# A graph-attention loop on one core: edge values and transposes amid TensorE's picks, one subtraction and the next terms an iteration later

## The chip, the core and the metric

The kernel runs on one core of a Trainium2 chip. A core has five engines that run side by side, each with its own queue of instructions in order: TensorE (PE in the profile; PEld is its weight load), VectorE (DVE), ScalarE (ACT), GpSimd (POOL) and SyncE (SP), which issues most of the DMAs. They share an on-chip memory (SBUF) and the accumulator banks of TensorE (PSUM), and wait for each other on semaphores. The metric is the device time of one execution in microseconds (us); it is the median of several runs.

## What is computed

The reference is one layer of attention over a graph with 6,250 nodes and 206,250 edges (sorted by their destination), 64 channels in 4 heads of 16, followed by a residual and a layer norm. Cut to its core:

```python
Qh = (x @ Wq.T + bq).reshape(n, H, D)
Kh = (x @ Wk.T + bk).reshape(n, H, D)
Vh = (x @ Wv.T + bv).reshape(n, H, D)
Ee = (edge_attr @ We.T + be).reshape(-1, H, D)
score = (Kh[src] * Qh[dst] * (1.0 / np.sqrt(D)) * Ee).sum(-1)
score = jnp.exp(jnp.clip(score, -5.0, 5.0))
msg = Vh[src] * score[..., None]
wV = jax.ops.segment_sum(msg, dst, num_segments=n)
x = _layernorm(x + wV.reshape(n, H * D))
```

So each edge needs the key and value row of its source, the query row of its destination and its own edge value; it makes a weight and a message, and the messages are summed at their destinations.

## The kernel before

The edges are cut into 1,612 tiles of 128, and 8 tiles make a group `g`; there are 202 groups. Two groups in a row make a step (the last 8 groups are steps of one). The main loop (L884) runs one iteration per group, and each iteration works on several groups at once, at different stages. The order of all instructions on all engines is written out by hand: each engine runs its own in program order. Adding a call earlier or later in the loop's body is what orders it against others on the same engine; between engines, waits follow from the tiles that are read and written.

The stages of a group, by function. All matmuls are issued through `product` (L690), so they share line L691 in the profile and are told apart by the tile they write.

- `edges` (L693, PE, room<-et): 8 matmuls that multiply edge features with the edge weights, into the upper part of the tile `room`. `biased` (L702, L706, ACT) adds the bias and copies them to SBUF as `eb`.
- `queries` (L709, PE, qq<-to,qw): the query rows of the destinations, by a matmul with one-hot columns that ACT builds (`onehot_rows`, L247, and `onehot_rows_rest`, L253).
- `terms` (L717, L721, DVE): query times edge value, `term`. `turn` (L723, L727, PE): its four transposes, into the tile `qe[g % 2]`.
- `products` (L742, DVE): L745 multiplies the keys with `qe`, L748 adds up per head: the score.
- `weigh` (L751, ACT): L754 and L756 clip and exponentiate it. The weights of a group are written into `room` as well.
- `message` (L758, L768, DVE): value times weight, written over `qe[g % 2]`. As the sums are to be exact in bfloat16 matmuls, the message is split into three parts: `keep` (L780, L782, ACT) copies what is left to bfloat16, `take` (L784, L787, DVE) subtracts that copy. So per group: keep 0, take 0 (the first subtraction, qe<-qe,msg), keep 1, take 1 (the second, msg<-qe,msg, which is the third part).
- `sums` (L799, PE, room<-msg,of): 16 matmuls, once per step, in even iterations, add the messages of a step at their destinations through a one-hot matrix (`onehot_edges`, L729, L737, DVE), into the `pa` part of `room`. `add` (L818, DVE, odd iterations): L822 adds the three parts up, L828 twice adds the sum to the node rows.

`room` (L615) is one PSUM tile of two banks. Edge values, sums, and the weights lie in it side by side, and accesses of different engines to it are ordered as accesses to the whole tile.

Key and value rows of the sources come in two ways. Most are gathered by POOL, one indirect DMA a tile (`gather`, L264, 1,320 in the run, 128 rows each). A batch of four tiles in about three iterations is fetched on TensorE instead: `hots` (L647, L651, DVE) makes one-hot blocks, `picks` (L661, PE, pick<-hot,parts) multiplies them with the table, three matmuls of 128x512 for each of 25 blocks. An iteration has 24 or 27 picks (33 blocks in four iterations). When a batch is complete, `picked` (L671, L673, DVE) masks it, `picked_kv` (L676, PE) multiplies it with the key and value weights and `place_kv` (L683, L686, ACT) copies it to its place. `by_two` (L656) gives the blocks of an iteration in twos. `mark` and `where` note matmuls of the iteration; the iteration's gathers are made to wait for these, spread over them.

In iteration `g` the order was, on each engine:

- PE: edges of g + 3, [picked_kv], all picks, transposes of g + 1, queries of g + 2, [sums, if g is even]
- DVE: products of g, first piece of one-hots, message of g, other pieces, first subtraction of g, [add, if g is odd], [picked], [one-hots of the step, if g is odd], second subtraction of g, terms of g + 2
- ACT: weights of g (L754, L756), bias of g + 3, L247, first copy of g, [place_kv], L253, second copy of g

The lines that set the order around the picks:

```python
                if g + 3 < NG:
                    edges(g + 3)
...
                for some in by_two(todo):
                    picks(some)
                    where.append(mark[-1])
                if g + 1 < NG:
                    turn(g + 1)
                if g + 2 < NG:
                    queries(g + 2)
```

The functions that the change touches, and what calls them:

## Time and profile before

| | before |
|---|---|
| median of 3 runs | 2070.77 us (2070.09 to 2071.17) |
| the profiled execution's own time | 2091.55 us |
| its span in the profile | 2089.7 us |
| mean granted TensorE clock | 0.946 |
| DVE, largest groups (busy) | L651 469.5, L768 139.9, L748 138.3, L787 139.3 and 137.0, L721 137.1, L745 137.2 us |
| PE, largest groups (busy) | picks 1110.1, sums 159.5, edge values 151.8, transposes 126.0 us |
| POOL | 1,320 gathers, 1248.4 us busy |
| DMA | 97 GB/s to and from HBM over the span |

The profile is one execution, recorded by the hardware; its time lies somewhat above the runs without a profile. A row of the timeline has the start, the duration, the engine, the line, the operation with what it writes and reads, its size, and in brackets how long the engine had been idle before it and what seems to have released it ("issue" where nothing recorded did). "xN" joins N instructions in a row into one line. The view of waits adds up such idle time by waiter and releaser. The view of windows gives, for a stretch of time, its length, each engine's busy time in it, the granted clock of TensorE as a share of full speed, the share of the DMA engines' time and GB/s. The ends of matmuls are modelled, so the start of the next is the better mark.

### The profile page before, as it was taken

How to read it: one execution, taken by the hardware profiler on the slowest of the kernel's cores; microseconds unless marked ns; L12 is line 12 of the kernel's file. 1: busy time of each engine (PE TensorE's matmuls, PEld its weight loads, DVE VectorE, ACT ScalarE, POOL GpSimd, SP SyncE). 2: the span in 40 equal slices, each digit the busy share in tenths (PEclk: the TensorE clock that was granted, in tenths of full speed). 3: DMA queues.
4: the chain of work that ended last, by engine and by line, in shares of the span. 5: the costliest groups of instructions: out<-in, count | busy, mean ns of one | idle time of the engine just before them, and what ended most of it. 6: DMA issues, size and time to landing. Idle time of an engine off the chain costs nothing.

```text
span 2089.7 us, 29080 instructions
## 1 busy us (share of the span) xinstructions
PE 1715.4 (82%) x9720; PEld 881.7 (42%) x9907; DVE 1563.1 (75%) x2484; ACT 995.5 (48%) x1712; POOL 1287.9 (62%) x1370
## 2 busy tenths in 40 slices
PE   6488798888888888888878888888888888878864
PEld 6244344444444444444434444444444443444432
DVE  5377777777777787777777778777877777778775
ACT  3454454445444455445444454444444544445553
POOL 6566666666666666666666666666666666666552
PEclk9789999999999999999999999999999999999975
DMA  6534333333333333333333333333333333333320
GB/s 174 191 92 117 89 99 100 84 101 101 81 102 85 102 97 86 102 92 102 100 82 100 96 93 102 83 99 102 82 111 90 98 101 82 101 87 95 95 81 24
DMA packets 115175, 203.87 MB, mean 98 GB/s; under 512 B 55427, under 2 KB 56175, under 8 KB 114901
## 3 DMA queue, kind: packets, MB, share of 16 engines
q1 hardware_dynamic: 71058, 112.94, 18.2%
q0 software_dynamic: 43520, 87.91, 16.5%
q8 instruction: 80, 1.31, 0.3%
q10 hardware_dynamic: 436, 1.04, 0.2%
q14 instruction: 81, 0.66, 0.1%
HBM read 194.18 MB, written 7.59 MB: 97 GB/s over the span
## 4 chain that ended last, share of the span: by engine, by line
PE 60%; DVE 14%; issue 11%; ACT 10%; another core or an unknown queue 2%; POOL 1%; DMA 1%; DVEq 0%; POOLq 0%; ACTq 0%; SPq 0%
PE pick L691 44%; PE room L691 12%; DVE hot L651 4%; ACT eb L706 3%; DVE qe L768 3%; DVE qe L787 2%; PE qe L727 2%; PE qq L691 1%; ACT room L756 1%; ACT to L253 1%; ACT to L247 1%; PE ps L467 1%; ACT msg L782 1%; POOL kv L264 1%
## 5 line engine op out<-in xcount | busy, mean ns | idle before, releaser
L264 POOL DMA_INDIRECT kv<-kv_tab,src_i x1320 | 1248.4, 946 | 747.1 <-issue 295.2
L691 PE MATMUL pick<-hot,parts 128*128 128x512 bf16 x4538 | 1110.1, 389 | 100.3 <-issue 88.0
L691 PEld LDWEIGHTS <-parts 128*128 128x128 bf16 x4725 | 455.2, 100 | 724.9 <-issue 270.6
L651 DVE TENSOR_TENSOR hot<-from,still 128x2560 bf16<-128x2560 bf16 (+4 forms) x411 | 469.5, 1149 | 0.0
L754 ACT ACTIVATE score<-score,five_p 128x32 f32<-128x32 f32 x202 | 64.9, 321 | 756.0 <-DVE score L748 419.8
L768 DVE SCALAR_TENSOR_TENSOR qe<-room,kv 128x512 f32<-128x512 f32 x200 | 139.9, 699 | 273.4 <-ACT eb L706 243.3
L691 PE MATMUL room<-et,we_sb 64*64 64x256 f32 (+1 forms) x1616 | 151.8, 428 | 141.3 <-DVE qe L787 33.0
L782 ACT ACTIVATE msg<-qe 128x512 bf16<-128x512 f32 x400 | 236.9, 592 | 7.0 <-DVE qe L787 4.3
L253 ACT ACTIVATE to<-to,one_p 126x1024 bf16<-126x1024 bf16 x198 | 227.3, 1148 | 0.0
L691 PE MATMUL room<-msg,of 128*128 128x192 bf16 x1592 | 159.5, 254 | 81.0 <-issue 26.9
L247 ACT ACTIVATE to<-kb,minus_row 126x1024 bf16<-126x1024 uint8 x198 | 224.8, 1135 | 0.0
L721 DVE TENSOR_TENSOR term<-eb,qq 128x512 f32<-128x512 f32 x202 | 137.1, 679 | 115.1 <-PE pick L691 35.3
L787 DVE TENSOR_TENSOR msg<-qe,msg 128x512 bf16<-128x512 f32 x200 | 137.0, 685 | 65.0 <-issue 28.0
L691 PEld LDWEIGHTS <-of 128*128 128x128 bf16 x1600 | 136.5, 101 | 107.8 <-issue 79.4
L756 ACT ACTIVATE room<-score,five_p 128x32 f32<-128x32 f32 x202 | 58.8, 291 | 232.4 <-PE pick L691 180.0
L706 ACT ACTIVATE eb<-room,be_col 128x512 f32<-128x512 f32 x202 | 138.6, 686 | 25.6 <-remote 15.9
L787 DVE TENSOR_TENSOR qe<-qe,msg 128x512 f32<-128x512 f32 x200 | 139.3, 696 | 6.9 <-ACT msg L782 3.6
L748 DVE TENSOR_REDUCE score<-prod 128x32 f32<-128x512 f32 x202 | 138.3, 684 | 7.0
L745 DVE TENSOR_TENSOR prod<-kv,qe 128x512 f32<-128x512 f32 x202 | 137.2, 679 | 5.3 <-issue 2.7
L727 PE MATMUL qe<-ident,term 128*128 128x128 f32 x806 | 126.0, 280 | 5.3 <-DVE term L721 4.9
L691 PEld LDWEIGHTS room<-et,we_sb 64*64 64x64 f32 x1616 | 49.1, 138 | 191.8 <-issue 125.9
L727 PEld LDWEIGHTS qe<-ident,term 128*128 128x128 f32 x806 | 102.7, 144 | 49.0 <-DVE term L721 9.6
(139 smaller groups left out, 972.5 us busy)
## 6 DMA issues: line engine op xcount, KB each, us to landing
et<-in_eT SPq DMA_DIRECT2D x100, 512.0 KB
kb<-key_tab SPq DMA_DIRECT2D x101, 252.0 KB
kv<-kv_tab,src_i POOLq DMA_INDIRECT x1320
srcs<-in_src_rows SPq DMA_DIRECT2D x63, 256.0 KB
qw<-q_tab SPq DMA_DIRECT2D x202, 15.8 KB
kv_tab<-kv_sb SPq DMA_DIRECT2D x4, 640.0 KB
q_tab<-q SPq DMA_DIRECT2D x5, 480.0 KB
y<-in_x_blocks SPq DMA_DIRECT2D x2, 512.0 KB
```

Source lines behind the costliest of these rows:

```text
L247: nc.scalar.activation(TO[g][:, :n, :], KB.pop(g)[:, :n * P].rearrange("p (j e) -> p j e", j=n), AF.Square, bias=minus_row3[:3 * W])
L253: nc.scalar.activation(TO[g][:, :n, :], TO[g][:, :n, :], AF.Relu, bias=one_p[:3 * W], scale=-1.0)
L264: return nc.gpsimd.indirect_dma_start(out=kv_of(g)[:, j, :], out_offset=None, in_=kv_tab[:, :], in_offset=bass.IndirectOffsetOnAxis(ap=src ...
L651: nc.vector.tensor_tensor(HOT[k][:, :hi - lo].rearrange("p b (a c) -> p b a c", c=2), pairs(FROM[m])[:, None].to_broadcast(shape), block2[ ...
L691: mark.append(nc.tensor.matmul(*aps, **kw))
L706: nc.scalar.activation(EB[g][:, :n].rearrange("p (i r) e -> p r i e", r=2), ee[:, :, :n // 2], AF.Identity, bias=be_col)
L727: nc.tensor.transpose(qe[g % 2][:, k:k + half + 1:half, :], TERM[g][:, k, :], ident)
L745: nc.vector.tensor_mul(prod[:, :n, :], kv_of(g)[:, :n, :C], qe[g % 2][:, :n, :])
L748: nc.vector.tensor_reduce(score, prod[:, :n, :].rearrange("p g (h d) -> p g h d", h=H), axis=AX.X, op=OP.add)
L768: nc.vector.scalar_tensor_tensor(to.rearrange("p g (h d) -> p g h d", h=H), WEIGHT.pop(g)[:, :, :, None].to_broadcast([P, n, H, D]), LEAST ...
L782: nc.scalar.activation(part, left, AF.Copy)
L787: nc.vector.tensor_sub(left if i == 0 else part_of(g, 2)[1], left, part)
```

## The change

In the loop, the order of the calls changes; the functions stay as they are.

- On PE, four blocks (12 picks) come first, then the edge values of g + 3, the transposes of g + 1 and the queries of g + 2, then the remaining picks, then the sums. `picked_kv`, where there is one, comes ahead of all.
- On DVE, after the products of g come the second subtraction of group g − 1 and the terms of g + 1, then the first piece of one-hots. The first subtraction of g comes last in the iteration, behind the add and the step's one-hots.
- On ACT, the second copy of g − 1 opens the iteration, ahead of the weights. The bias is added to the edge values of g + 2, computed an iteration before.
- Ahead of the loop, the groups 0 to 2 are prepared as this order needs it.

```diff
-            for g in range(2):
-                edges(g)
-                biased(g)
-                queries(g)
-                terms(g)
+            edges(0)
+            biased(0)
+            queries(0)
+            terms(0)
             turn(0)
+            edges(1)
+            biased(1)
+            queries(1)
             edges(2)
-            biased(2)
...
                 parted = now and step_of[g] < WHOLE
+                former = before and step_of[g - 1] < WHOLE
                 fetch_blocks(g)
                 where.append(mark[-1])
-                if g + 3 < NG:
-                    edges(g + 3)
+                if former:
+                    keep(g - 1, 1)
                 if now:
                     products(g)
+                if former:
+                    take(g - 1, 1)
+                if g + 1 < NG:
+                    terms(g + 1)
+                if now:
                     weigh(g)
-                if g + 3 < NG:
-                    biased(g + 3)
+                if g + 2 < NG:
+                    biased(g + 2)
                 for mc in ahead[:1]:
                     hots(*mc)
...
                 for mc in ahead[1:]:
                     hots(*mc)
-                if parted:
-                    take(g, 0)
                 for s in done:
                     add(s)
...
-                for some in by_two(todo):
+                two = by_two(todo)
+                for some in two[:2]:
                     picks(some)
                     where.append(mark[-1])
+                if g + 3 < NG:
+                    edges(g + 3)
                 if g + 1 < NG:
                     turn(g + 1)
                 if g + 2 < NG:
                     queries(g + 2)
+                for some in two[2:]:
+                    picks(some)
+                    where.append(mark[-1])
                 where.append(mark[-1])
                 if g - 1 in ends and now:
                     sums(ends[g - 1])
                 if g + 4 < NG:
                     onehot_rows_rest(g + 4)
-                if parted:
-                    keep(g, 1)
...
                 if parted:
-                    take(g, 1)
-                if g + 2 < NG:
-                    terms(g + 2)
+                    take(g, 0)
```

## The prediction

> **What bounds the kernel now.** I read the page first, then the list of waits, then the timeline of one pair of iterations, then windows of it.
>
> ```profile
> span 2089.7 us, 29080 instructions
> PE 1715.4 (82%) x9720; PEld 881.7 (42%) x9907; DVE 1563.1 (75%) x2484; ACT 995.5 (48%) x1712; POOL 1287.9 (62%) x1370
> PE 60%; DVE 14%; issue 11%; ACT 10%; another core or an unknown queue 2%; POOL 1%; DMA 1%; DVEq 0%; POOLq 0%; ACTq 0%; SPq 0%
> L691 PEld LDWEIGHTS <-parts 128*128 128x128 bf16 x4725 | 455.2, 100 | 724.9 <-issue 270.6
> L782 ACT ACTIVATE msg<-qe 128x512 bf16<-128x512 f32 x400 | 236.9, 592 | 7.0 <-DVE qe L787 4.3
> ```
> ```profile
> L768 DVE SCALAR_TENSOR_TENSOR qe<-room,kv x200: 698/700/700, 105.7 to 2069.6; 128x512 f32<-128x512 f32 x100
> ```
> PE carries 60% of the chain of waits, DVE 14% and ACT 10%: PE is the bound, but a handshake with the other two adds to it. L768 runs once an iteration: (2069.6 − 105.7)/199 = 9.87 us, 19.74 us a pair (odd iteration, then even). The loop has 4725 picks, in the code 33 × 3 in four iterations, or 24.75 each: 4725/49.5 = 95 full pairs.
>
> ```profile
> DVE qe L768 <- ACT eb L706: 243.3, 105, 6.6
> POOL kv L264 <- PE pick L691: 239.7, 194, 2.4
> ACT room L756 <- PE pick L691: 180.0, 88, 5.7
> ```
> Here (waiter, releaser: total us, times, longest) is the handshake. L756, which writes the weights into the tile `room`, waits 2.0 us a time (180.0/88) for a PE signal, and L768 then waits 2.3 (243.3/105) behind it. The timeline of one pair shows why (start, duration, what; the idle time before in brackets):
>
> ```profile
> 1061.04 0.41 PE L691 MATMUL qq<-to,qw 126*64 126x512 bf16 x2
> 1061.37 1.49 PE L691 MATMUL room<-msg,of 128*128 128x192 bf16 x16
> 1062.80 0.66 PE L691 MATMUL room<-et,we_sb 64*64 64x256 f32 x8
> 1063.12 0.69 DVE L721 TENSOR_TENSOR term<-eb,qq 128x512 f32<-128x512 f32 x1 [0.24 <-PE room L691]
> ...
> 1063.72 0.68 DVE L745 TENSOR_TENSOR prod<-kv,qe 128x512 f32<-128x512 f32 x1
> ...
> 1064.44 0.69 DVE L748 TENSOR_REDUCE score<-prod 128x32 f32<-128x512 f32 x1
> 1065.04 1.48 DVE L651 TENSOR_TENSOR hot<-from,still 128x2560 bf16<-128x2560 bf16 x1
> ...
> 1067.62 0.29 ACT L756 ACTIVATE room<-score,five_p 128x32 f32<-128x32 f32 x1 [2.14 <-PE pick L691]
> ...
> 1067.94 0.69 ACT L706 ACTIVATE eb<-room,be_col 128x512 f32<-128x512 f32 x1
> ...
> 1068.66 0.70 DVE L768 SCALAR_TENSOR_TENSOR qe<-room,kv 128x512 f32<-128x512 f32 x1 [2.14 <-ACT eb L706]
> ...
> 1069.27 0.94 DVE L651 TENSOR_TENSOR hot<-from,still 128x1536 bf16<-128x1536 bf16 x1
> ...
> 1070.19 0.70 DVE L787 TENSOR_TENSOR qe<-qe,msg 128x512 f32<-128x512 f32 x1
> ...
> 1070.80 0.35 DVE L822 TENSOR_REDUCE room<-room 128x64 f32<-128x192 f32 x1
> ...
> 1071.39 0.28 DVE L828 SCALAR_TENSOR_TENSOR y<-room,below,y 128x64 f32<-128x64 f32 x1
> ...
> 1071.81 0.66 PE L691 MATMUL room<-et,we_sb 64*64 64x256 f32 x8 [1.33 <-DVE qe L787]
> 1072.40 4.86 PEld L691 LDWEIGHTS <-parts 128*128 128x128 bf16 x24 [0.38 <-issue]
> ...
> 1077.60 0.60 PE L727 MATMUL qe<-ident,term 128*128 128x128 f32 x4
> ...
> 1078.12 0.76 PE L691 MATMUL qq<-to,qw 126*64 126x512 bf16 x2
> ...
> 1078.58 0.29 ACT L756 ACTIVATE room<-score,five_p 128x32 f32<-128x32 f32 x1 [2.19 <-PE pick L691]
> ...
> 1080.38 1.48 PE L691 MATMUL room<-msg,of 128*128 128x192 bf16 x16 [1.49 <-DVE qe L768]
> 1081.79 0.66 PE L691 MATMUL room<-et,we_sb 64*64 64x256 f32 x8
> ```
> The edge values (room<-et) take 0.59 to the next PE work (1071.81 to 1072.40), so in the odd iteration they end at 1063.39; yet L756, which needs them, starts at 1067.62, 4.23 later; in the even iteration they end at 1072.40 and L756 starts at 1078.58, 6.2 later. This late arrival I call the lag. From L756 the chain L706, L768, hot, L787, sum, add takes 1071.81 − 1067.62 = 4.19 to the next edge values, which may not overwrite the tile before. Lag and chain together just outlast the 24 picks: PE idles 1.33 there, and 1.49 before the sums for L768. The lag is not constant:
>
> ```profile
> 1980.27 0.66 PE L691 MATMUL room<-et,we_sb 64*64 64x256 f32 x8
> ...
> 1982.29 0.29 ACT L756 ACTIVATE room<-score,five_p 128x32 f32<-128x32 f32 x1
> ```
> ```profile
> 1972.00:2000.00 28.00, 27.79 (x173) 14.62 (x174) 24.18 (x36) 14.70 (x26) 11.18 (x12) 1.00 0.33 87
> 1200.00:1600.00 400.00, 340.08 (x1965) 170.57 (x2003) 313.32 (x479) 197.46 (x330) 252.92 (x268) 0.97 0.35 97
> ```
> Near 1980, with POOL's gathers sparse (11.18 us busy of 28), L756 starts 2.02 after the edge values' start, 1.4 after their end, and waits for nothing: PE is busy 27.79 of 28. Over 1200 to 1600, POOL is busy 63% and PE 85%.
>
> **The change part by part.** No instruction is added or removed; the built order keeps each kind's count. What moves:
>
> *Edge values amid the picks.* Before, edge values open the iteration, with 24 picks of cover for the L756–L828 chain. Now 12 picks come first, then edge values (g+3), transposes, queries, and 12 or 15 more picks. They must still wait for the add (odd iterations) or L768 (even). One pick takes (1077.60 − 1072.40)/24 = 0.217 us, so the cover falls from 5.2 to 2.60 us. Edge values 0.59 (1071.81 to 1072.40), transposes 0.52 (1077.60 to 1078.12), queries 0.35 (by starts, 1061.04 to 1061.37): 1.46. Later picks 12.75 × 0.217 = 2.76. Sums 1.43 (1061.37 to 1062.80).
>
> *L756 no longer needs this iteration's edge values.* In an even iteration these are half an iteration old: free. In an odd one L756 now follows the sums, the last PE work of the iteration before, on the same tile. What queues behind L756 on ACT: L706, L247, the first bfloat16 copy L782; DVE's L768 waits for it, and all behind L768, the add included, which releases the edge values. So the chain keeps its PE signal, from sums instead of edge values, 1.5 us earlier, while its end is needed at 12 picks instead of 24.
>
> *First subtraction last.* L787 (0.61, 1070.19 to 1070.80) leaves the chain between L768 and add: 4.19 − 0.61 = 3.58.
>
> *Second subtraction and terms an iteration later.* They go to DVE behind the products: L787 0.61 and L721 0.60 (1063.12 to 1063.72), ahead of the first hot. The sums and transposes that need them come over 2.6 us later; no wait there. The products L745 now wait for transposes issued in the middle of the previous iteration; behind L745 stands all of DVE.
>
> *The rest.* Bias L706 moves to older edge values, the second copy ahead of L754 on ACT: 48% busy, hidden by DVE's products; without that cover 0.59, a copy's 592 ns, an iteration. Gathers wait on other marks of PE's order; none is added, and POOL is 62% busy; SP's DMAs keep their order. Cost nothing.
>
> *The lag's price.* No row shows L756 waiting for sums. Bounds: 1.4 (1980) and 6.2 (even row). From the sums' end (1062.86, start plus duration) to L756's start stand 4.76, between the odd row's 4.23 and 6.2: I take 4.76. For transposes to L745 the nearest row is queries' end 1061.45 to L721 at 1063.12: 1.67; bounds 0.3 (in the sparse window, an estimate from PE busy 27.79 of 28: no wait is left) and 6.2.
>
> *Sum.* Odd iteration, from the end of the sums: 4.76 + 3.58 = 8.34 to edge values, where 12 picks cover 2.60; PE stalls 5.74. Then 1.46 + 2.76: 12.56. Even iteration: the transposes ended 0.35 + 2.76 = 3.11 before it starts; DVE starts 1.67 after them, then L745 0.72, L748 0.60, L787 0.61, L721 0.60, hot 1.40 (1.48 less the 0.08 by which starts overlap), L768 0.70, signal 0.14 (1071.67 to 1071.81): 6.44 − 3.11 = 3.33 to edge values (cover 2.60, stall 0.73), then 1.46 + 2.76 + 1.43: 8.98. Pair 21.54 against 19.74: +1.80, times 95 = +171 us. The quoted pair (1062.80 to 1081.79) takes 18.99, 0.75 under the mean, for batches' products and source work that I take as lost in the stall; if not, +71 more. The profiled execution took 2091.55 us (span 2089.7 and 1.85 around it), 20.78 over the median 2070.77; the difference carries over: 2070.8 + 171 = 2242.
>
> **The rivals.** *Signals on time, faster.* The pair is 7.80 + lag of the sums, plus 7.31 + lag of the transposes (at least its own work, 6.82 + 1.43 = 8.25, as soon as that lag is under 0.94). It beats 19.74 when the two lags sum to less than 4.63 (6.43 taken). Halved, 2.38 and 0.84: 10.18 + 8.25 = 18.43, −1.31 × 95 = −124: 1946. For: 1972 to 2000; sums are earlier than edge values were. Against: POOL's 63% in the long window, and L756's lag of 4.23 and 6.2 in a common pair.
>
> *The clock falls.*
> ```profile
> 1095.52 1.13 PE L691 MATMUL room<-et,we_sb 64*64 64x256 f32 x8 [3.08 <-DVE room L822]
> 1096.59 8.19 PE L691 MATMUL pick<-hot,parts 128*128 128x512 bf16 x26
> 1104.62 0.60 PE L727 MATMUL qe<-ident,term 128*128 128x128 f32 x4
> ```
> ```profile
> 1096.00:1098.00 2.00, 2.00 (x12) 0.59 (x5) 2.00 (x4) 0.00 (x0) 1.39 (x3) 0.50 0.37 61
> ```
> After 3.08 idle the granted clock is 0.50: 27 picks took 8.03, 0.297 each, and edge values 1.13 instead of 0.66. An odd stall of 5.74 would bring it each pair: 12.75 × 0.08 = 1.02 on the later picks, 0.47 on edge values, about 0.5 on transposes and queries (the same ratio, an estimate): 2.0 × 95 = +190: 2432. Against: the sum's stall is an average, and the lag may shrink first. The Trainium skill, "TensorE: Matmul & The Clock Gate", section "What's actually happening", puts the fall to half rate after an idle window of about 3.4 us and the return after about as much sustained work; the row agrees, at 3.08 us, and by that rule 2432 would be the time.
>
> *The lag shrinks as POOL gets room.* POOL's gathers are fixed, so a longer iteration leaves it more idle; with lags of 4.0 and 1.2, 11.80 + 8.51 = 20.31, +0.57 × 95 = +54: 2125. For: the contrast of the two windows.
>
> *The change doesn't do what it says* (no edge values moved, no wait changed): the built order shows both moved; within 0.2%.
>
> **How the numbers follow.** Forecast (2170 to 2330): 0.42. Clock (to 2450): 0.20. Smaller lag (2075 to 2170): 0.16. Faster (1850 to 2066): 0.18. No change: 0.04. A measurement tells 0.2%, 4 us, from nothing: faster 0.18, same 0.04, slower 0.78. The range leaves out the faster half of the fast case and the tail of the clock's: 2000 to 2430; the likeliest one's own range is 2170 to 2330.
>
> **What would show it.** Right: an odd iteration near 12.6 us and an even one near 9; PE idle 4 to 6 us before the odd edge values, released by the add; L756 in odd iterations released by the sums. Wrong: L756 starting within 3 us of the sums' end; L745 late by more than 3 us; a mean granted clock well under 0.95 (then the clock's rival); PE's busy share over 82%.

## The result, and the profile after

The changed kernel takes 2097.38 us (median of 4 runs, 2095.77 to 2100.46) beside 2070.97 us for the kernel before (2070.09 to 2071.64): a ratio of 1.013, 95% interval 1.0112 to 1.0147. It is 26 us slower; 171 us were forecast. A ratio can differ a little from that of the medians, since it leaves out executions in a slower state (one of four of the kernel without marks below). Two more comparisons of the same two kernels gave 1.0151 (1.013 to 1.0173) and 1.014 (1.0118 to 1.0162).

The page of the profile of the kernel after, its first lines, the chain by engine, and three groups (busy, mean ns; idle time just before, and what ended it):

```profile
span 2095.1 us, 29075 instructions
PE 1754.0 (84%) x9907; PEld 875.6 (42%) x9907; DVE 1546.8 (74%) x2484; ACT 1020.4 (49%) x1712; POOL 1287.9 (61%) x1370
...
PE 65%; DVE 18%; ACT 7%; issue 7%; another core or an unknown queue 1%; DMA 1%; POOL 0%; ACTq 0%; SPq 0%; DVEq 0%; POOLq 0%
...
L691 PE MATMUL pick<-hot,parts 128*128 128x512 bf16 x4725 | 1139.3, 396 | 0.7 <-issue 0.4
...
L745 DVE TENSOR_TENSOR prod<-kv,qe 128x512 f32<-128x512 f32 x202 | 138.3, 685 | 358.5 <-PE pick L691 250.8
L691 PE MATMUL room<-et,we_sb 64*64 64x256 f32 (+1 forms) x1616 | 146.8, 435 | 277.9 <-ACT to L253 90.2
```
The same three groups in the kernel before (the record of 187 of its picks is missing from the trace):

```profile
L691 PE MATMUL pick<-hot,parts 128*128 128x512 bf16 x4538 | 1110.1, 389 | 100.3 <-issue 88.0
...
L691 PE MATMUL room<-et,we_sb 64*64 64x256 f32 (+1 forms) x1616 | 151.8, 428 | 141.3 <-DVE qe L787 33.0
...
L745 DVE TENSOR_TENSOR prod<-kv,qe 128x512 f32<-128x512 f32 x202 | 137.2, 679 | 5.3 <-issue 2.7
```
The stalls changed place. Ahead of the products L745 stood 5.3 us in the whole run before, now 358.5; ahead of the edge values 141.3, now 277.9; ahead of picks 100.3, now 0.7. The waits of the kernel after (waiter, releaser: us in total, times, longest):

```profile
POOL kv L264 <- PE pick L691: 330.9, 213, 8.0
...
DVE prod L745 <- PE pick L691: 250.8, 107, 5.4
...
PEld room L691 <- DVE qe L768: 114.5, 56, 6.0
ACT room L756 <- PE room L691: 111.1, 52, 3.9
...
DVE qe L768 <- ACT eb L706: 34.5, 25, 6.7
```
L768 behind L706 has all but gone (243.3 to 34.5); L756 waits for `room` (the sums) in place of the picks that followed the edge values. Both are as the prediction has them. The size is not, and the timeline of one pair shows where (start, duration, what, idle time before):

```profile
1058.91 0.66 PE L727 MATMUL qe<-ident,term 128*128 128x128 f32 x4
...
1059.83 3.41 PE L691 MATMUL pick<-hot,parts 128*128 128x512 bf16 x15
1060.38 0.94 POOL L264 DMA_INDIRECT kv<-kv_tab,src_i  x1 [0.30 <-issue]
...
1062.67 0.69 DVE L745 TENSOR_TENSOR prod<-kv,qe 128x512 f32<-128x512 f32 x1 [3.97 <-PE pick L691]
...
1063.02 0.94 POOL L264 DMA_INDIRECT kv<-kv_tab,src_i  x1 [1.70 <-PE pick L691]
1063.08 1.48 PE L691 MATMUL room<-msg,of 128*128 128x192 bf16 x16
...
1064.40 2.75 PE L691 MATMUL pick<-hot,parts 128*128 128x512 bf16 x12
...
1064.66 0.29 ACT L756 ACTIVATE room<-score,five_p 128x32 f32<-128x32 f32 x1 [0.23 <-ACT score L754]
...
1066.59 0.69 DVE L768 SCALAR_TENSOR_TENSOR qe<-room,kv 128x512 f32<-128x512 f32 x1
...
1068.64 0.28 DVE L828 SCALAR_TENSOR_TENSOR y<-room,below,y 128x64 f32<-128x64 f32 x1
...
1069.02 0.66 PE L691 MATMUL room<-et,we_sb 64*64 64x256 f32 x8 [1.86 <-ACT to L253]
...
1070.50 0.94 POOL L264 DMA_INDIRECT kv<-kv_tab,src_i  x1 [0.31 <-issue]
1070.53 4.86 PEld L691 LDWEIGHTS <-parts 128*128 128x128 bf16 x24 [0.23 <-issue]
...
1073.02 0.69 DVE L745 TENSOR_TENSOR prod<-kv,qe 128x512 f32<-128x512 f32 x1 [2.03 <-PE pick L691]
...
1073.40 0.94 POOL L264 DMA_INDIRECT kv<-kv_tab,src_i  x1 [1.95 <-PE pick L691]
...
1077.68 0.66 PE L691 MATMUL room<-et,we_sb 64*64 64x256 f32 x8 [1.79 <-DVE qe L768]
```
The sums end at 1064.40, where the picks begin, and L756 starts 0.26 later; 4.76 was taken. The odd stall is 1.86, not 5.74. (The releaser named there, L253, is the last to finish by the profile; the edge values wait for the add, which ends at 1068.92, and follow it by 0.10.) The products do come late: 3.1 us after the transposes in the first iteration (1059.57 to 1062.67), 2.75 in the second (1070.27 to 1073.02). Both times they start within 0.4 us of a gather that had waited for TensorE too.

Over groups 10 to 189 the waits that the prediction priced are, in mean us, worked out from each record's start and end in the trace (the two iterations of a pair apart):

```
                                     before          after
                                  odd    even     odd    even
edge values' end to L756         4.34    5.22      -       -
sums' end to L756                  -       -     0.71      -
transposes' end to L745          4.21    4.82     2.22    2.45
L756 behind L748's end           1.92    1.22     2.18    0.43
L768 to the next edge values     3.48    3.20     2.69    1.23
stall ahead of edge values       1.15    0        1.62    0.95
```
The last row is the stall ahead of the edge values that come next after the iteration's L768. In 73 of the 90 odd iterations of the kernel after, L756 starts more than 0.25 us behind L754, so with these late signals, too, it mostly waits for the sums. From the first picks of an iteration to those of the next, an odd iteration takes 9.56 us and an even one 10.48; 12.56 and 8.98 were forecast.

Where TensorE's own time went, from the start of the first pick to the end of the last (each group up to the start of the next; "between" is idle time of over 0.1 us between groups, and "inside" is such idle time within groups, which their columns contain):

```
          picks  edge v. transp. queries  sums  batches  between    sum   inside
before   1170.9    135.5   101.5    75.0  150.8    94.0    166.5  1894.3   104.5
after    1119.5    122.9   126.9    74.0  141.1    81.3    242.9  1908.7    10.4
```
Idle time between groups rose by 76 us, and idle time inside them fell by 94. Without any idle time TensorE's work takes 32 us more, 25 of it in the transposes. That makes 14 us. The medians differ by 26; the profiled execution of the kernel before lay 20.6 us above its median, the one after within its runs. The gain inside the groups is not the clock's:

```profile
200.00:1900.00 1700.00, 1471.93 (x8429) 715.83 (x8428) 1285.52 (x1978) 835.45 (x1367) 1068.36 (x1132) 0.94 0.35 95
```
```profile
200.00:1900.00 1700.00, 1445.93 (x8329) 724.98 (x8493) 1309.59 (x1989) 819.99 (x1375) 1074.79 (x1138) 0.97 0.35 95
```
After, then before; the third number from the end is the granted clock, and it is lower after the change. By the trace's record of the clock it fell to half 58 times in the run after and 33 times before. In these 1,700 us TensorE was at work at half clock for 190 us after and 93 before, which costs at most half of that time, 95 and 47 us.

### The profile page after: what moved, and what is told of

It is laid out like the page before. It is cut to its first block, busy times and chain, and to the rows that moved or that the text cites. A ratio compares the mean times of both kernels' runs of the same rounds, so it can differ in the third digit from the quotient of the medians.

```text
span 2095.1 us, 29075 instructions
## 1 busy us (share of the span) xinstructions
PE 1754.0 (84%) x9907; PEld 875.6 (42%) x9907; DVE 1546.8 (74%) x2484; ACT 1020.4 (49%) x1712; POOL 1287.9 (61%) x1370
## 4 chain that ended last, share of the span: by engine, by line
PE 65%; DVE 18%; ACT 7%; issue 7%; another core or an unknown queue 1%; DMA 1%; POOL 0%; ACTq 0%; SPq 0%; DVEq 0%; POOLq 0%
PE pick L691 43%; PE room L691 11%; PE qe L727 6%; DVE hot L651 5%; PE qq L691 3%; DVE prod L745 3%; DVE score L748 3%; DVE qe L768 2%; DVE msg L787 2%; DVE term L721 2%; ACT to L253 2%; ACT to L247 2%; ACT eb L706 1%; ACT msg L782 1%
## 5 line engine op out<-in xcount | busy, mean ns | idle before, releaser
L691 PE MATMUL pick<-hot,parts 128*128 128x512 bf16 x4725 | 1139.3, 396 | 0.7 <-issue 0.4
L691 PEld LDWEIGHTS <-parts 128*128 128x128 bf16 x4725 | 461.1, 101 | 586.1 <-issue 142.4
L745 DVE TENSOR_TENSOR prod<-kv,qe 128x512 f32<-128x512 f32 x202 | 138.3, 685 | 358.5 <-PE pick L691 250.8
L691 PE MATMUL room<-et,we_sb 64*64 64x256 f32 (+1 forms) x1616 | 146.8, 435 | 277.9 <-ACT to L253 90.2
L782 ACT ACTIVATE msg<-qe 128x512 bf16<-128x512 f32 x400 | 237.6, 594 | 275.9 <-DVE qe L787 127.0
L754 ACT ACTIVATE score<-score,five_p 128x32 f32<-128x32 f32 x202 | 64.9, 321 | 519.5 <-DVE score L748 468.0
L253 ACT ACTIVATE to<-to,one_p 126x1024 bf16<-126x1024 bf16 x198 | 226.6, 1144 | 0.0
L768 DVE SCALAR_TENSOR_TENSOR qe<-room,kv 128x512 f32<-128x512 f32 x200 | 138.8, 694 | 101.1 <-issue 42.3
L727 PE MATMUL qe<-ident,term 128*128 128x128 f32 x806 | 151.2, 317 | 15.9 <-issue 13.2
L691 PE MATMUL room<-msg,of 128*128 128x192 bf16 x1592 | 155.3, 250 | 10.4 <-issue 9.9
L756 ACT ACTIVATE room<-score,five_p 128x32 f32<-128x32 f32 x202 | 58.8, 291 | 186.0 <-PE room L691 111.1
L706 ACT ACTIVATE eb<-room,be_col 128x512 f32<-128x512 f32 x202 | 138.6, 686 | 22.2 <-PE room L691 8.0
L748 DVE TENSOR_REDUCE score<-prod 128x32 f32<-128x512 f32 x202 | 138.3, 684 | 7.0
L727 PEld LDWEIGHTS qe<-ident,term 128*128 128x128 f32 x806 | 96.3, 156 | 103.3 <-issue 99.9
```

What stands on the lines that cost most here:

```text
L253: nc.scalar.activation(TO[g][:, :n, :], TO[g][:, :n, :], AF.Relu, bias=one_p[:3 * W], scale=-1.0)
L691: mark.append(nc.tensor.matmul(*aps, **kw))
L727: nc.tensor.transpose(qe[g % 2][:, k:k + half + 1:half, :], TERM[g][:, k, :], ident)
L745: nc.vector.tensor_mul(prod[:, :n, :], kv_of(g)[:, :n, :C], qe[g % 2][:, :n, :])
L748: nc.vector.tensor_reduce(score, prod[:, :n, :].rearrange("p g (h d) -> p g h d", h=H), axis=AX.X, op=OP.add)
L768: nc.vector.scalar_tensor_tensor(to.rearrange("p g (h d) -> p g h d", h=H), WEIGHT.pop(g)[:, :, :, None].to_broadcast([P, n, H, D]), LEAST ...
```

## The experiments

Each experiment ran beside the kernel before, on the same chip. Four of the six comparisons, the one of the result among them, had the kernel before at 2070 to 2092 us; in the other two the very same program took 1728.8 and 1729.7 us. I call these "with the lag" and "without the lag", for reasons that the experiments give; all ratios are to the kernel before in the same comparison. Lines in profiles of edited kernels can be one or two lower than in the tables above.

### Parts of the change (with the lag, before 2092.1 us)

TensorE's part alone:

```diff
-                if g + 3 < NG:
-                    edges(g + 3)
...
-                if g + 3 < NG:
-                    biased(g + 3)
...
-                for some in by_two(todo):
+                two = by_two(todo)
+                for some in two[:2]:
                     picks(some)
                     where.append(mark[-1])
+                if g + 3 < NG:
+                    edges(g + 3)
+                    biased(g + 3)
                 if g + 1 < NG:
                     turn(g + 1)
                 if g + 2 < NG:
                     queries(g + 2)
+                for some in two[2:]:
+                    picks(some)
+                    where.append(mark[-1])
```


> Only TensorE's order is changed: the first 12 picks, then edge values (with their bias behind them on ACT), transposes, queries, then the other picks; DVE and ACT keep the order of the kernel before, so the first subtraction is still ahead of the add. Theory A (cover: what the change costs is the cover, 12 picks instead of 24 for the chain from L756 to the add): the whole of the cost and more, since the 0.61 us of the first subtraction is in the chain, 0.61 x 95 = 58 us above the changed kernel, near 2155 us. Theory B (the lag of TensorE's signals depends on when the gathers pause, not on the signal): L756 waits for no edge values of its own iteration any more, so it starts on time, and the kernel is between before and after, 2060 to 2100 us.

Measured: 2256.96 us, 1.0805 (1.0771 to 1.0839). Both theories missed. Its waits name the reason:

```profile
DVE msg L787 <- ACT msg L782: 488.4, 174, 7.9
...
ACT eb L706 <- PE pick L691: 260.1, 53, 7.7
```
The bias still belongs to the edge values of the same iteration, which now come in the middle of the picks. ACT stands at L706 for their late signal, the second copy L782 stands behind it, and DVE stands at the second subtraction (488.4 us in all). So the moves are not a sum of parts. In the whole change the bias belongs to older edge values and the second copy comes an iteration later; without these two, edge values amid the picks cost far more. Which of the two counts, no run tells.

DVE's and ACT's part alone, TensorE in its old order (bias stays at g + 3, with a third `eb` buffer):

```diff
+                if former:
+                    keep(g - 1, 1)
                 if now:
                     products(g)
+                if former:
+                    take(g - 1, 1)
+                if g + 1 < NG:
+                    terms(g + 1)
+                if now:
                     weigh(g)
...
-                if parted:
-                    take(g, 0)
...
-                if parted:
-                    keep(g, 1)
...
                 if parted:
-                    take(g, 1)
-                if g + 2 < NG:
-                    terms(g + 2)
+                    take(g, 0)
```


> Only DVE's and ACT's order is changed: second copy, second subtraction and terms an iteration later, first subtraction last; TensorE keeps its order (edge values, all picks, transposes, queries), bias and edge values stay as in the kernel before. Theory A (cover): the chain from L756 to the add is 0.61 us shorter with the full cover of 24 picks, and faster by what the stall ahead of odd edge values allows, up to 0.61 x 95 = 58 us: 2013 to 2060 us. Theory B: L756 still waits for edge values that arrive with the gathers' pause, 4 to 5 us late; the 1.2 us moved ahead of the one-hots are hidden by that, so 2030 to 2075 us. Against both: products wait for the transposes at the end of the iteration before, and then 1.2 us more stand between them and the message: slower, over 2090 us.

Measured: 2087.29 us, 0.9972 (0.9959 to 0.9985): 5 us faster. The odd stall fell from 1.15 to 0.84 us, about half of the 0.61 us that left the chain. This part of the change alone is a small gain.

### The lag taken away (before 2092.1 us)

```diff
-        return nc.gpsimd.indirect_dma_start(
-            out=kv_of(g)[:, j, :], out_offset=None, in_=kv_tab[:, :],
-            in_offset=bass.IndirectOffsetOnAxis(ap=src_i[:, t:t + 1], axis=0))
+        return nc.sync.dma_start(out=kv_of(g)[:, j, :], in_=kv_tab[t % 40 * P:t % 40 * P + P, :])
```
In the kernel before:

> The kernel before with each of the 1,320 gathers on GpSimd replaced by a plain DMA of 128 consecutive rows of the same table to the same place, issued by SP (so the rows are the wrong ones; waits and bytes stay). Theory B (TensorE's signals are late because gathers run back to back): edge values to L756 under 1 us, TensorE busy over 95%, about 8.3 us an iteration as in the window from 1972 to 2000 us: 2071 - 200 x 1.55 = about 1760 us. Rival (the lag belongs to TensorE's signals as such): lag of 4 to 5 us stays and the time is within 3% of 2071.

In the kernel after:

> The changed kernel with the same replacement of its 1,320 gathers. Theory B: no lag, so the odd stall is 0.3 + 3.58 - 2.60 = about 1.3 us a pair and the rest is TensorE's own work: 1.3 x 95 = up to 120 us above the kernel before with the same replacement, or less where the picks of a batch cover it: 1760 to 1880 us. Rival (the lag belongs to the signals): within 3% of 2097.

Measured: 1741.45 us, 0.8321 (0.8303 to 0.8338), and 1810.86 us, 0.8654 (0.8639 to 0.8668). Both kernels came out near theory B's times (about 1760, and 1760 to 1880 us). The lag needs the gathers: without them, L756 follows L748 in 0.39 us in odd iterations of the kernel before (1.92 with them), and TensorE is busy nearly throughout (before, plain rows; engine busy, share of the span):

```profile
PE 1614.3 (93%) x9720; PEld 864.1 (50%) x9907; DVE 1555.8 (89%) x2484; ACT 995.2 (57%) x1712; POOL 39.4 (2%) x50
```
And with no lag, the change costs 69 us (1810.86 − 1741.45), more than with it. Waits of the kernel after, plain rows (L754 is here the line that writes the weights):

```profile
ACT room L754 <- PE room L689: 263.0, 100, 3.3
```
and one odd iteration of it:

```profile
905.61 1.48 PE L689 MATMUL room<-msg,of 128*128 128x192 bf16 x16
907.15 2.54 PE L689 MATMUL pick<-hot,parts 128*128 128x512 bf16 x11
907.20 0.29 ACT L754 ACTIVATE room<-score,five_p 128x32 f32<-128x32 f32 x1 [2.65 <-PE room L689]
...
910.57 0.28 DVE L826 SCALAR_TENSOR_TENSOR y<-room,below,y 128x64 f32<-128x64 f32 x1
...
910.95 0.66 PE L689 MATMUL room<-et,we_sb 64*64 64x256 f32 x8 [1.26 <-ACT to L253]
```
The weights wait 2.65 us for the sums, 0.05 us behind whose end they start. From there to the edge values 3.75 us pass, and 12 picks cover 2.6 of them. In all 100 odd iterations the weights wait for the sums. This is the stall that the prediction describes, at a lag of almost nothing. Idle time on TensorE is 35 us in the loop of the one kernel and 105 in that of the other.

### No marks for the gathers

```diff
             ins = gather_kv(g, j)
-            if j == js[0]:
-                behind(ins, after)
```
In the kernel after:

> The changed kernel with the gathers waiting for no mark in TensorE's order any more; they wait only for their own data and place. Theory B (signals come in when a train of gathers pauses, and the pauses are made by the marks): with no marks the gathers run on until the place they write is still read, the pauses fall elsewhere and less often, and TensorE's signals come later: slower than the changed kernel by 1 to 5%. Rival (only the number of gathers counts, not where they pause): within 0.5% of the changed kernel.

In the kernel before:

> The kernel before with the gathers waiting for no mark in TensorE's order. Theory B: as with the changed kernel, slower by 1 to 5%, with edge values to L756 longer than the 4.3 to 5.2 us of before. Rival: within 0.5% of before.

Measured without the lag (before 1728.77 us): 1797.49 us, 1.040 (1.0383 to 1.0418), and 1730.08 us, 1.0006 (0.9996 to 1.0015). There the marks do nothing, although the gathers run and run back to back. So gathers alone don't make the lag; something else must be added, which the profiles don't show. It is not the chip alone: the comparison of the parts, with the lag, and the last one below, without it, are both on record under the same chip number, 7. The run of the kernel before was repeated where the lag is:

> The kernel before with gathers that wait for no mark, a second time, for a chip with the lag (without it 1.0006 times before). If the pauses that the marks make let TensorE's signals through, there are fewer of them and signals come later: 1.01 to 1.05. If the marks' pauses only hold the gathers up and set the pace, the time falls: 0.95 to 0.99. If neither, within 0.5%.

Measured with the lag (before 2071.55 us): 2367.44 us, 1.1365 (1.1316 to 1.1414): far over the worst expected. Its waits and a piece of its timeline:

```profile
POOL kv L264 <- DVE qe L766: 629.0, 127, 10.5
```
```profile
1203.46 0.94 POOL L264 DMA_INDIRECT kv<-kv_tab,src_i  x1 [2.08 <-DVE qe L766]
...
1212.20 0.94 POOL L264 DMA_INDIRECT kv<-kv_tab,src_i  x1 [0.30 <-issue]
...
1214.92 0.29 ACT L754 ACTIVATE room<-score,five_p 128x32 f32<-128x32 f32 x1 [5.48 <-remote]
...
1216.94 0.94 POOL L264 DMA_INDIRECT kv<-kv_tab,src_i  x1 [3.79 <-DVE qe L766]
```
Eight gathers run in one train from 1203.46 to 1213.14. The weights, which wait for TensorE, start 1.8 us after its end, and the next train waits for their message. The signal came in the pause.

One mark an iteration:

```diff
-                    gather((lot, where[i * len(where) // len(going)]))
+                    gather((lot, where[0]))
```


> The kernel before with both lots of an iteration's gathers behind the first mark, the last matmul of the iteration before, so one wait an iteration instead of two. With the lag, if each pause costs the pace of the gathers about 1.3 us and there are 1.2 an iteration: 6.53 x 1.25 + 1.3 = 9.5 us an iteration, 0.96 of before. If it is the signals that count, they come once an iteration instead of 1.2 times: 1.00 to 1.03. On a chip without the lag: within 0.5%.

Measured with the lag: 2237.62 us, 1.0795 (1.0753 to 1.0836). Both forecasts missed. The "two" of the expectation is mistaken: in the kernel before each gather has a mark of its own, six to eight an iteration. So the series is: a mark for each gather 1, one for an iteration 1.08, none 1.137. Holding the gathers up is not what costs. That too few pauses do fits the series, and is argued: between 150 and 1950 us the gathers run in 227 trains (runs without a pause) in the kernel before, in 139 with one mark and in 142 with none.

TensorE's semaphore events in the trace bear on this. They are fewer than its signals (1,877 for 2,037 in the kernel before), so they are a sample. Counted by where they fall, between 150 and 1950 us (to 1600 without the lag; a train is a run of gathers less than 1.6 us apart, its slots are 1.25 us long, a pause begins 1.9 us after the last gather's start): events for each us spent in that place

```
                             slot 1     2     3     4     5     6     7   8 on  pause
before, with the lag           0.76  1.26  0.63  0.35  0.35  0.24  0.15   0.13   5.08
after, with the lag            0.96  1.09  0.64  0.52  0.30  0.41  0.38   0.19   5.04
before, no marks, with         0.33  0.42  0.52  0.29  0.23  0.24  0.17   0.11   1.04
before, no marks, without        -     -     -     -     -     -     -    0.77     -
before, a mark moved, without    -     -     -     -     -     -     -    1.21     -
```
With the lag, events come at the start of a train, hardly at its end, and in numbers in the pause: in the kernel before 801 of 1,694 fall into 158 us of pauses. Without the lag the gathers hardly ever pause, and events come all the same (the last row is the kernel before with one mark moved, from the last section of experiments).

The place in a train does not decide alone whether a signal is late. In the kernel after, the sums end 1.25 to 2.5 us into a train in 36 of the 90 odd iterations, and L756 follows after 0.25 us in the mean. In the kernel before, the edge values end at the same place in 21 of 90, and L756 follows after 6.18 us, behind the train's end. Why the one signal passes and the other does not is open.

### The weights in a tile of their own

```diff
-            weights = [room[:, 1, 2 * P + C + k * G * H:2 * P + C + (k + 1) * G * H]
-                       .rearrange("p (g h) -> p g h", g=G) for k in range(3)]
+            weights = [accp.tile([P, G, H], F32, name=f"weight{k}") for k in range(3)]
```
In the kernel after, without the lag:

> The changed kernel with the weights in a tile of their own in SBUF, so that L756 waits neither for the sums nor for edge values, and edge values no longer wait for L768. Theory C (what the change costs is the wait of L756 for the sums on the shared tile, 2.2 us behind L748 in odd iterations instead of 0.4, with 12 picks of cover behind it): 1.8 us less in the odd chain and no even stall, 1 to 2 us a pair: 95 to 190 us faster than the changed kernel, 1.00 to 0.92 of the kernel before. Rival (the pace of the gathers and their pauses sets the iteration): stalls only move, within 1% of the changed kernel.

and with the add moved up behind the terms:

```diff
                 if g + 1 < NG:
                     terms(g + 1)
+                for s in done:
+                    add(s)
                 if now:
                     weigh(g)
...
-                for s in done:
-                    add(s)
```


> As the one before, and the add goes to DVE directly behind the terms, ahead of the one-hots, the message and all else. Theory C: the edge values then wait only for sums, products and add, ahead of the 12 picks' end: no stall ahead of edge values (under 0.3 us an iteration); 0.2 to 0.6 us a pair faster still than with the own tile alone. Rival (pace of the gathers): the same time as with the own tile alone within 0.5%.

Measured: 1744.92 us, 1.0098 (1.0081 to 1.0114), and 1744.75 us, 1.0094 (1.0077 to 1.0111). Against the changed kernel without marks in the same comparison (1797.49; in the kernel before, marks make no difference there) the own tile saves 53 us, and the idle time ahead of edge values falls from 91 to 23 us in the loop: without the lag the wait on the shared tile is the change's loss, all but 16 us. Theory C had the cause right and its size (95 to 190 us) too large; the rival's 1% failed. The page of the profile of the kernel after with its own tile:

```profile
span 1741.5 us, 28771 instructions
...
PE 1648.2 (95%) x9907; PEld 847.6 (49%) x9907; DVE 1536.3 (88%) x2484; ACT 1010.0 (58%) x1712; POOL 1309.0 (75%) x1370
```
With most idle time gone, TensorE's work itself has grown by 23 us in the loop, beside the kernel before without marks: the picks take 1048 us against 1026 and the transposes 112 against 101, the sums and queries 11 us less. Each iteration now switches from picks to edge values, which is part of it: in the medians, a pick or a transpose starts 0.22 us after the pick ahead of it, edge values 0.31 us. Moving the add has no effect, though 0.2 to 0.6 us a pair were forecast: hardly a stall was left.

With the lag, the same kernel again, and the tile in the kernel before and in the DVE part:

> The changed kernel with the weights in a tile of their own, a second time, for a chip with the lag. Without the lag it took 1.0098 times before. Theory B and C: with the lag, L756 was at most 1.8 us late in odd iterations for the sums, and the even edge values 0.95 us late: 1 to 2 us a pair less than the changed kernel, 0.93 to 0.97 times before. Rival (pace of the gathers and their pauses): 1.00 to 1.02 times before.

> The kernel before with the weights in a tile of their own in SBUF: L756 follows L748 in 0.4 us without a wait for edge values, L768 without a wait for the bias L706; edge values wait for add and bias only. Theory B: on a chip with the lag the odd stall ahead of edge values goes (1.15 us an iteration pair) and so does the wait for L768 ahead of the sums: 3 to 8% faster than before; on a chip without it the stall of 0.3 us is all there is: 0 to 2% faster. Rival (the pace of the gathers and their pauses sets the iteration): within 1% on both.

> DVE's and ACT's part of the change alone (second copy, second subtraction and terms an iteration later, first subtraction last; TensorE in the order of before) with the weights in their own tile. Theory B: as the kernel before with its own tile, with the odd chain 0.61 us shorter and the products later by their wait for transposes: within 1% of that kernel. Against it: where products wait for transposes that end an iteration only 0.4 us before it, DVE is late by the lag: 2 to 5% slower than that kernel on a chip with the lag.

Measured (before 2070.01 us): 2082.21 us, 1.0066 (1.0032 to 1.0101); 2064.35 us, 0.9975 (0.9965 to 0.9984); 2055.96 us, 0.9933 (0.9916 to 0.9949). The forecast of several per cent for the first two failed, and the rival held; the third came within 1% of the second, as forecast. The changed kernel took 2102.6 us in this comparison (below), so the own tile saves 20 us of its 33 us of loss here. But the odd stall ahead of edge values stays, at 1.58 us against 1.61: L756 waits for no sums any more, and now the add waits for the bias, which shares `room` and stands behind a late signal (no such row of L822 behind L706 is among the waits of the changed kernel):

```profile
DVE room L821 <- ACT eb L705: 77.9, 38, 5.5
```
In the DVE part with its own tile the idle time between TensorE's groups is 38 us in the loop instead of 167, yet the picks take 1171 us as before, the sums 218 instead of 151 and the batches 114 instead of 94. With the lag, much of the time taken out of the waits between groups comes back inside the groups. The waits of matmuls into `room`, sums and edge values, for nothing that is recorded grow (this kernel, then the kernel before):

```profile
PE room L690 <- issue: 59.3, 89, 1.9
```
```profile
PE room L691 <- issue: 36.7, 51, 2.7
```
A part of it is the clock, 0.924 in the mean against 0.946.

The DVE part with its own tile ran once more:

> DVE's and ACT's part with the weights in their own tile, a second time. On a chip without the lag: TensorE's own work is all that is left, in one group of picks an iteration: 0.975 to 1.00 of before. With the lag: 0.990 to 0.997 again.

Measured with the lag (before 2071.55 us): 2060.95 us, 0.995 (0.9933 to 0.9967). With the lag it is the fastest kernel here, 0.5 to 0.7% ahead of the kernel before; it wasn't run where there is no lag.

### The changed kernel again, and the marks it moved

> The changed kernel once more, beside the kernel before on the same chip; the chips differ: the kernel before took 1728.8 us on one of them, where TensorE's signals are not late, and 2071 and 2092 us where they are. Theory B and C together: on a chip without the lag the change costs its whole loss of cover, as with plain row loads (1.04 times the kernel before there), near 1795 us; on a chip with the lag 1.01 to 1.015 times before. Rival (the change costs the same share whatever the lag): 1.013 on any chip.

> The changed kernel once more. On a chip where TensorE's signals are not late: 1.035 to 1.045 times before by the loss of cover, as with plain row loads; on a chip with the lag 1.010 to 1.018. Rival (same share on any chip): 1.013.

Both comparisons had the lag: 2102.6 us, 1.0151, and 2100.76 us, 1.014. So the changed kernel as it stands was never seen without the lag.

The change leaves `where.append(mark[-1])` at its place, and so the mark that stood behind the queries now stands behind the last picks, twice. (The second mark of an iteration, which stood behind the edge values, now repeats the first one unless a batch comes between; no run put that one back.) Put back behind the queries:

```diff
                 if g + 2 < NG:
                     queries(g + 2)
+                where.append(mark[-1])
                 for some in two[2:]:
                     picks(some)
                     where.append(mark[-1])
-                where.append(mark[-1])
```


> The changed kernel with the mark behind the queries put back behind the queries (in the change it lands behind the last picks, where it repeats the mark before it), so that gathers wait for TensorE some 100 times more in the run. Theory B (each wait of a gather lets TensorE's late signals through): products start earlier after the transposes than 2.2 to 2.5 us, and the time is 0.985 to 1.005 of before with the lag. Theory A (cover alone): 1.013 to 1.015, as the changed kernel. Without the lag both give the changed kernel's time.

and in the kernel before the first mark behind the edge values:

```diff
-                where.append(mark[-1])
                 if g + 3 < NG:
                     edges(g + 3)
+                where.append(mark[-1])
```


> The kernel before with the first mark of an iteration behind the edge values instead of ahead of them, so that the first gather waits for them and their signal comes in that pause. Theory B: edge values to L756 falls from 4.3 to 5.2 us to under 3.5, and the time is 0.96 to 0.99 of before with the lag. Rival (what counts is how many waits the gathers have, of which this has some 75 fewer): 1.00 to 1.03.

Measured without the lag (before 1729.7 us): 1795.48 us, 1.0384 (1.0367 to 1.0401), and 1729.58 us, 1.0001 (0.9991 to 1.001). Neither question is answered, as both are about the lag. The first run is the nearest that there is to the changed kernel without it: 66 us slower than before, with 103 us of idle time in TensorE's loop against 37 in the other kernel of this comparison, 66 us more.

## Why the prediction was right or wrong

**The mechanism: right, and the direction in part by luck.** The odd edge values wait for a chain that starts at the sums' end, because the weights share `room`, and 12 picks cover too little of it. Without gathers the weights wait for the sums in 100 iterations, and without the lag the own tile takes 53 of 69 us back. With the lag, L756 waits for the sums in 73 of 90 odd iterations, but there the own tile only hands the stall on to the bias. The luck: with nothing but the lags put right, the prediction's formulas give 7.80 + 0.71 + 7.31 + 2.45 = 18.27 us a pair, faster than the 19.74 of before.

**The chain's pieces: near.** L756 to edge values in odd iterations was put at 3.58 us; the trace has 1.28 to L768 and 2.69 on, 3.97. Products to L768 in even ones: 3.93 put, 3.82 measured. For the cover, 2.60 us of picks, the plain-row timeline has 2.54.

**The lag's price: the step that failed.** The sums' lag was taken as 4.76 us, from a row in which L756 waited for the edge values that follow the sums. It measured 0.71 in the mean, so the odd stall is 1.62 instead of 5.74 us, 4.1 us of the pair. A lag read off one signal does not belong to another: at the same place in a train of gathers the sums' signal came after 0.25 us and the edge values' after 6.18. The bounds, 1.4 and 6.2, did not hold it. The transposes' 1.67, against 2.22 and 2.45, was near enough.

**TensorE's own work: too small, and it hid part of the error.** In the forecast's pair of 21.54 us, 6.47 are stalls (5.74 + 0.73) and 15.07 are TensorE's work. Measured, over 95.45 pairs (4725/49.5), are 2.54 of idle time between groups and 17.45 of work, 20.0 in all. So the stalls were put 3.9 us too long and the work 2.4 too short: 1.0 in the picks (0.237 us each instead of 0.217; 282 of them ran at half clock), 0.85 in the batches' products, which were taken as lost in the stall, and 0.5 in the other matmuls. Without the lag the formulas fit: 7.80 + 0.10 + 8.25 + 0.86 = 17.0 us against 17.2 in the changed kernel without marks, where the kernel before takes 16.4.

**The signs on record.** Of the signs of being wrong, three came: L756 within 3 us of the sums' end (0.71), a granted clock under 0.95 (0.925), and PE's busy share over 82% (84%).

**The parts at nothing.** No run prices the older bias and the later second copy alone. That at least one of them is needed, the prediction does not say: TensorE's part without both costs 8%. The gathers' marks were put at nothing too, though two of them came to repeat others; with the lag this was not measured.

**The rivals.** *Signals on time, faster* was wrong in kind: in the kernels nearest to the changed one, where signals are on time, the loss is largest, 4%, since the kernel before gains more from that. *The clock falls* came in part: 282 picks ran at half clock after and 160 before, and the clock's cost rose by at most 48 us, where the rival had 190. It is no more than a part, since without the lag the clock is 0.98 and the loss 66 to 69 us. *The lag shrinks* gave 2125 us with a range of 2075 to 2170 and came nearest. The smaller lag is there, but not by its reason: the gathers' pauses are 158 us before and 166 after.

**What stays open.** With the lag, the change costs 76 us of idle time between TensorE's groups and gets 94 back inside them. That late signals also hold TensorE itself up is argued, not shown; it fits that in the kernel before 56 of the 90 us of such gaps in picks and sums end in the gathers' pauses, which are 158 of 1,800 us. Open are also why the sums' signal passes where the edge values' does not, whether the repeated marks cost something with the lag, and what makes the lag at one time and not at another.

## What to carry to other kernels

Before pricing a wait by a delay that a profile shows, make sure that the delay is that signal's own: here, at the same place in a train of gathers, one signal from TensorE to ScalarE came after 0.25 us and another after 6.18. When several values share one PSUM tile, moving one of them moves the waits of all: an own tile for the weights took 53 of 69 us back where nothing else was in the way. Add up an engine's work from the same trace as its waits: here the work was put 2.4 us a pair too low, and that hid part of a stall put 3.9 too high. And where something else paces the whole schedule, stalls removed at one place return at another; measure more than once, and on more than one chip, before counting them as won.

## What the runs showed of the hardware that was not expected

- One and the same program took 1729 us in two comparisons and 2070 to 2092 us in four others, 20% apart, each time within 0.3% inside the comparison, and under one chip number both ways. The gathers last the same in both (946 and 947 ns).
- In the slower comparisons TensorE's semaphore events come at 0.1 to 1.3 for each us while indirect gathers run back to back, and at 5 in the pauses (kernels before and after). Of two TensorE signals at the same place in a train, one came after 0.25 us and the other after 6.18. VectorE's signal to ScalarE (L748 to L754) came in 0.03 us in the midst of such trains (end at 1065.13, start at 1065.16 in the pair of the prediction).
- Waits that hold gathers up can make a kernel faster: with the lag, none at all cost 13.7%, one an iteration 8%.
- With the picks of an iteration in two groups, and transposes behind edge values, TensorE's picks and transposes took 22 and 12 us more in some 190 iterations, and its sums and queries 11 less, with hardly a wait in sight (own tile, without the lag).
